# Flamingo gated layer: both kinds of scores in three stretches a step, one pool of two-bank PSUM slots

## The chip, the cores and the metric

The kernel runs on one core of a Trainium2 chip. The metric is the device time of one execution in microseconds; the median of the runs is compared. The core's engines are TensorE (PE, with its weight loads as PEld), VectorE (DVE), ScalarE (ACT), GpSimd (POOL) and SyncE (SP, which issues the DMAs). TensorE writes to PSUM, eight banks of 2 KB on each of 128 partitions; ACT and DVE read it out.

## The reference

A gated layer of cross-attention and a feed-forward part (FFN) with quantised weights, for 32 batches of 224 tokens of width 512, with 750 context tokens of width 384; 16 heads of 32:

```python
q = (x @ Wq.T).reshape(B, N, H, d).transpose(0, 2, 1, 3)
kv = (y @ Wkv.T).reshape(B, N2, 2, H, d).transpose(2, 0, 3, 1, 4)
attn = jnp.einsum('bhnd,bhmd->bhnm', q * scale, k)
attn = jnp.where(pad_mask[:, None, :, None], attn, jnp.float32(-1000000000.0))
attn = jax.nn.softmax(attn, axis=-1)
out = jnp.einsum('bhnm,bhmd->bhnd', attn, v)
...
x = x + jnp.tanh(g_xattn[0]) * _L0_xattn_ref(_layernorm(x, axis=-1), ctx_768, ...)
x = x + jnp.tanh(g_ffn[0]) * _L0_ffn_ref(_layernorm(x, axis=-1), ...)
```

The FFN is two linear layers (512 to 2048 and back) with a GELU between. Before each, the activations are RMS-normalised and rounded to a grid of 127 steps of their row's maximum; the weights are rounded to -1, 0 and 1 times their mean magnitude.

## The kernel before

**Steps.** The attention goes through 128 steps (`steps`, L189): a batch `b` and a group `g` of four heads. The four heads lie on four groups of 32 partitions, so that TensorE can work on the four at once, each with 32 rows of its array.

The softmax needs each row's maximum before the exponential, so the scores are computed twice, in two layouts:
- `maxima(b, g, i)` (L323), i = 0 to 2: scores with queries on the partitions (`sm`), 112 queries by 500 keys for each of four heads. DVE takes the maximum over the keys from PSUM into `mx`. After i = 2, `minus_max` (L350) makes of it the negative maximum in three bf16 parts (`nb`) with six small DVE operations, and `turn_max` (L369) turns these with two transposes on TensorE (`pn`); ACT copies the result to `nT`.
- `weights(b, g, u)` (L380), u = 0 to 2: scores with keys on the partitions (`se`), two chunks of 125 keys by 224 queries for each of four heads. Four small products with ones put the negative maximum into PSUM first, then eight products add the scores. ACT takes the exponential of all four banks in one instruction into `p`; POOL adds up `p` into `acc` (the softmax's denominators over the chunks).

`values` (L413) multiplies `p` with V into `po`, `sums` (L427) adds the denominators beside it, DVE transposes it and takes the reciprocal (`oT`, `rd`), `finish` (L447) scales on POOL and `store` (L488) writes to DRAM (`o_d`) with four DMAs.

**Fillers.** Between the score groups stand other units on TensorE: `k_units` (L275; a half of the K projection each, tile `pk`, read out by ACT), `v_piece` (L291; a piece `pv_None` or half a piece `pv` of the V projection, read out by ACT or DVE), `q_piece` (L262; `pq`, read out by DVE), and the FFN of the tokens that are through with attention: `b_matmul` (tile `ph`, first layer, read out by DVE) and `c_matmul` (tile `po2`, second layer, shown as `po<-w2q,hT`, called c below).

**Slots.** The loop over the steps (L1193) cuts each into six slots k. In an even slot stands `maxima` of the next step, in an odd one `weights` of this step, and after each the units put into that slot: first those marked as quick, then what `Ffn.fill` (L1011) picks from the FFN, then the rest. `fill` takes FFN units, in their order and with minimum distances in slots, as long as estimates of their time on PE, ACT and DVE fit into the slot's room (`PE_ROOM`, L1190). During the first steps `weight_units` (L498) take the place of the FFN: they read the FFN weights and quantise them. What is left of the FFN at the end goes out in an order worked out by `drain` (L1049). Every engine runs its instructions in the order in which this program issues them.

**PSUM.** Two pools share the eight banks:

```python
ps_s = pool("ps_s", 1, PSUM)     # L173: one slot, 4 banks: sm or se
ps_m = pool("ps_m", 4, PSUM)     # L174: four slots, 1 bank: all other units
```

So `sm` and `se` use one slot in turn: each has to wait until the engine that reads the other is through.

Of the kernel before, what the change touches and what calls it, by code (L numbers as in the profile page):

```python
# [9 lines left out]
F32 = mybir.dt.float32  # L10
# [15 lines left out]
def flamingo_gated_layer(  # L26
# [30 lines left out]
    P = 128  # L57
# [112 lines left out]
    smf = pool("smallf", 3)  # L170
    fp = pool("f", 1)
    htp = pool("hT", 2)
    ps_s = pool("ps_s", 1, PSUM)  # L173
    ps_m = pool("ps_m", 4, PSUM)  # L174

    wq_sb = wp.tile([P, NDC, D], F32, name="wq_sb")
# [143 lines left out]
        [(1, MQ, M, 0)],  # L320
    ]

    def maxima(b, g, i):  # L323


        qT, kT = q_of[b], k_of[b, g]
        if i == 0:
            mx_of[b, g] = smp.tile([CP, HG, 4], F32, tag="mx", name=f"mx_{b}_{g}")
        mx = mx_of[b, g]
        s = ps_s.tile([P, HG, 512], F32, tag="s", name=f"sm_{b}_{g}_{i}")  # L330
        for t, lo, hi, col in TAKES[i]:
            for j in range(HG):
                rows = slice(j * DH, (j + 1) * DH)
                pe.matmul(
                    s[:CP, j, col : col + hi - lo],
                    qT[rows, g, t * CP : (t + 1) * CP], kT[rows, lo:hi],
                    start=True, stop=True,
                )
        if i == 1:
            dve.tensor_reduce(  # L340
                mx[:, :, 1:3], s[:CP, :, : 2 * MQ].rearrange("p j (a n) -> p j a n", a=2),
                AX.X, ALU.max,
            )
        else:
            at = 3 * (i // 2)
            dve.tensor_reduce(
                mx[:, :, at : at + 1], s[:CP, :, : 2 * MQ].unsqueeze(2), AX.X, ALU.max
            )

    def minus_max(n):  # L350

# [28 lines left out]
    def weights(b, g, u):  # L380


        qT, kT, nT = q_of[b], k_of[b, g], nT_of[b, g]
        s = ps_s.tile([P, HG, 512], F32, tag="s", name=f"se_{b}_{g}_{u}")
        for j in range(HG):
            pe.matmul(
                s[:KC, j, : 2 * S].rearrange("p (i n) -> p i n", i=2),
                ones3[j * DH : j * DH + 3, :KC],
                nT[j * DH : j * DH + 3, :].unsqueeze(1).to_broadcast([3, 2, S]),
                start=True, stop=False,  # L390
            )
        for i in range(2):
            c = 2 * u + i
            for j in range(HG):
                rows = slice(j * DH, (j + 1) * DH)
                pe.matmul(
                    s[:KC, j, i * S : (i + 1) * S],
                    kT[rows, c * KC : (c + 1) * KC], qT[rows, g, :],
                    start=False, stop=(i == 1),
                )  # L400
# [97 lines left out]
    def weight_units():  # L498
# [27 lines left out]
        def mean():  # L526
            pm = ps_m.tile([P, 512], F32, tag="m", name="pwm")
            pe.matmul(pm[:, 0:2], ones, tot, start=True, stop=True)
            held["pm"] = pm

        def scales():
            pm = held.pop("pm")
# [26 lines left out]
        for n, wi in enumerate(every):  # L559
            def two(n=n, wi=wi):  # L560
                if n + 1 < len(every):
                    fetch(*every[n + 1], "wb")
                if n == 0:
                    scales()
                quantise(*wi)
            units.append(two)
        return units
# [37 lines left out]
    def ffn_units(i):  # L605
# [326 lines left out]
        "top": [[("PE", 0.3), ("ACT", 0.4)]],  # L932
# [15 lines left out]
    LAST = {  # L948
        name: [(NF, at) for at in after.split()]
        for name, after in {  # L950
            "w0": "top", "w1": "w0", "w2": "w1", "val": "", "fin0": "val", "sto0": "fin0",
            "vlast": "w2 val fin0", "fin1": "vlast fin0", "fin2": "vlast fin0",
        }.items()
    }
# [3 lines left out]
    class Ffn:  # L958
# [52 lines left out]
        def fill(self, rooms, stored, newest=False):  # L1011


            rooms, some = list(rooms), False
            rooms[0] += self.late(stored, 0 if rooms[0] >= 0.3 else 2)
            while True:
                if self.next < NF and (self.next + 1) * TG * P <= stored * S:
                    if len(self.parts) <= 2 * TG:
                        self.parts += [[self.next, part] for part in ffn_units(self.next)]
                        self.next += 1  # L1020
                found = next(
                    (
                        (p, u)
                        for p in (self.parts[::-1] if newest else self.parts)
                        for u in p[1]
                        if all(not us or min(us, most) <= room
                               for us, most, room in zip(u[3:6], (0.3, 9.0, 9.0), rooms))
                        and self.ready(p[0], u)
                    ),
                    None,  # L1030
                )
# [6 lines left out]
                some |= unit[3] > 0  # L1038
# [3 lines left out]
            return some  # L1042

        def late(self, stored, more):

# [135 lines left out]
    minus_max(0)  # L1181
    first_k = k_units(*steps[2])
    first_k[0]()

    ffn = Ffn()
    wunits = weight_units()
    LATE = 3
    PE_ROOM = 2.5, 1.9  # L1190
    v_left = [(b, hv, i) for b in range(B) for hv in range(2) for i in range(NKC // 2)]
    V_MORE = {0: 2, 2: 1, 3: 1, 4: 1}
    for n in range(N - 1):  # L1193
        b, g = steps[n]
# [32 lines left out]
        if n in V_MORE:  # L1227
            put_values(V_MORE[n])
        if n == 0:
            put(3, 1.7, lambda: centre(2 * P, D))  # L1230
        if n < 2:
            put(5, 1.5, q0[n + 2])
# [5 lines left out]
        more = b + 1 < B  # L1238
# [8 lines left out]
        if more and g > 1:  # L1247
            put(3, 1.5, qs[2 * g - 4])
            put(5, 1.5, qs[2 * g - 3])
        for k in range(6):  # L1250
            if k % 2 == 0:
                maxima(*nxt, k // 2)
            else:
                if k == 3 and last:
                    finish(*last)
                weights(b, g, k // 2)
            if k == 4:
                minus_max(n + 1)

            used = sum(us for us, _ in slots[k])  # L1260
            early = [unit for us, unit in slots[k] if unit in quick]
            for unit in early:
                unit()
            if wunits:
                if k in (1, 3, 5):
                    wunits.pop(0)()
            else:
                ffn.closing = n == N - 2 and k > 2
                some = ffn.fill(
                    (PE_ROOM[k % 2] - used, (1.1, 2.2)[k % 2], 1.7),  # L1270
                    (n - (k < 5)) // NG if n else 0,
                )
                if k == 0 and not some and lent is not None:

                    v_piece(*lent, 0)
                    slots[4] = [
# [5 lines left out]
                    unit()  # L1282
    last = steps[-2:]
    ffn.drain(
        [("top", 0, None, 0, 0, 0, lambda: turn_max(N - 1))]
        + [(f"w{u}", 0, None, 0, 0, 0, lambda u=u: weights(*last[1], u)) for u in range(3)]
        + [
            (name, 0, None, 0, 0, 0, lambda do=do, at=at: [f(*at) for f in do])
            for name, at, *do in (
# [44 lines left out]
```

## Time and profile before

| | |
|---|---|
| median of 3 runs | 2983.3 us (2980.32 to 2983.55) |
| profiled execution: span | 2983.6 us, granted TensorE clock 0.993 |
| PE busy | 2892.7 us, 97% |
| DVE, ACT, POOL busy | 1737.2, 1414.2, 2084.4 us |
| DMA | 189.80 MB, mean 64 GB/s |
| exponential `p<-se` | 384 times, mean 1663 ns |
| reduction `mx<-sm` | 384 times, mean 2243 ns |

The span is the time from the first to the last instruction of one profiled execution. Matmuls are pipelined and their ends are modelled: each is shown some 0.2 us longer than it holds up the next, so busy PE time hides short waits. The distance between the starts of neighbouring groups in the timeline is the safer measure. A group's line gives: line, engine, operation, output<-inputs, shapes, count, busy time and mean time of one, and the engine's idle time ahead of it with what ended most of it. A wait's line gives: who waited for whom, total us, times, longest. A timeline's line gives start and length in us. Most instructions go through one helper that records their order, so they all carry its line, L53, and the tiles' names tell them apart. An f32 matmul is recorded as two.

### The profile page before, as it was taken

What the parts mean: (1) busy time and instruction counts of PE and PEld (TensorE: products, weight loads), DVE (VectorE), ACT (ScalarE), POOL (GpSimd) and SP (SyncE); (2) the same over time, 40 slices, a digit from 0 to 9 for tenths busy, and PEclk for the clock granted to TensorE, in tenths of its full rate; (3) what the DMA queues carried; (4) which work ended last, traced back from release to release, by engine and by line L of the source; (5) the groups of instructions that cost most, each with busy time, mean ns of one, the idle gap of its engine ahead of it and who ended that gap; (6) DMA issues with size and microseconds to landing.
All of it is one profiled execution on the core that took longest, in us unless ns stands there. A gap on an engine that the chain in (4) does not pass through costs nothing.

```text
span 2983.6 us, 62984 instructions
## 1 busy us (share of the span) xinstructions
PE 2892.7 (97%) x26814; PEld 1840.7 (62%) x26814; DVE 1737.2 (58%) x2616; ACT 1414.2 (47%) x1438; POOL 2084.4 (70%) x2723
## 2 busy tenths in 40 slices
PE   8999999999999999999999999999999999999985
PEld 5666566666666666666666666666666666666653
DVE  5566555555556565555555565655655655556556
ACT  2344454544545455445445454544544554545444
POOL 3566767767766876777667777767767777777675
PEclk9999999999999999999999999999999999999998
DMA  5433222223222222222232212123122132222123
GB/s 148 106 99 98 55 50 73 43 62 75 42 61 61 52 55 73 69 44 48 63 73 47 65 40 80 48 62 74 45 50 62 45 71 67 50 71 48 39 52 78
DMA packets 375785, 189.80 MB, mean 64 GB/s; under 512 B 282160, under 2 KB 339920, under 8 KB 375376
## 3 DMA queue, kind: packets, MB, share of 16 engines
q1 hardware_dynamic: 375504, 185.79, 25.6%
q8 instruction: 209, 3.42, 0.5%
q14 instruction: 72, 0.59, 0.1%
HBM read 119.74 MB, written 29.27 MB: 50 GB/s over the span
## 4 chain that ended last, share of the span: by engine, by line
PE 82%; ACT 10%; POOL 3%; DVE 2%; issue 1%; DMA 1%; POOLq 0%; SPq 0%; ACTq 0%; DVEq 0%
PE po L53 17%; PE pk L53 15%; PE se L53 14%; PE sm L53 13%; PE pv_None L53 8%; ACT p L53 7%; PE pv L53 6%; PE ph L53 6%; PE pq L53 3%; DVE mx L53 2%; ACT L53 2%; POOL acc L53 1%; ACT h L53 1%; PE pn L53 1%; POOL h L53 1%
## 5 line engine op out<-in xcount | busy, mean ns | idle before, releaser
L53 POOL TENSOR_TENSOR acc<-acc,p 125x896 f32<-125x896 f32 x510 | 1066.9, 2092 | 324.8 <-ACT p L53 303.6
L53 DVE TENSOR_REDUCE mx<-sm 112x4 f32<-112x2000 f32 (+1 forms) x384 | 861.2, 2243 | 669.3 <-PE sm L53 669.2
L53 ACT ACTIVATE p<-se 125x1792 f32<-125x1792 f32 x384 | 638.8, 1663 | 760.6 <-PE se L53 706.9
L53 PE MATMUL pk<-y,wkv_sb 128*128 128x375 f32 x1536 | 541.6, 488 | 1.5 <-DMA y<-in_ctxT 1.5
L53 PE MATMUL sm<-kT,qT 32*112 32x500 f32 (+1 forms) x4096 | 426.9, 508 | 31.6 <-ACT p L53 22.7
L53 POOL TENSOR_TENSOR acc<-p 125x896 f32<-125x896 f32 x128 | 268.3, 2096 | 240.3 <-ACT p L53 237.1
L53 PEld LDWEIGHTS pk<-y,wkv_sb 128*128 128x128 f32 x1536 | 279.2, 190 | 175.7 <-issue 36.9
L53 PE MATMUL se<-qT,kT 32*125 32x224 f32 x6144 | 359.9, 348 | 0.0
L53 PE MATMUL po<-p,v 125*32 125x224 f32 x6144 | 317.1, 354 | 0.0
L53 PE MATMUL pv<-wkv_sb,y 128*125 128x256 f32 x1248 | 311.0, 385 | 0.0
L53 PEld LDWEIGHTS se<-qT,kT 32*125 32x125 f32 x6144 | 295.4, 183 | 0.1
L53 PEld LDWEIGHTS sm<-kT,qT 32*112 32x112 f32 x4096 | 159.3, 170 | 190.6 <-ACT p L53 137.6
L53 PEld LDWEIGHTS po<-p,v 125*32 125x32 f32 x6144 | 186.5, 110 | 118.9 <-issue 43.1
L53 PEld LDWEIGHTS pv<-wkv_sb,y 128*125 128x125 f32 x1248 | 223.3, 188 | 52.3 <-issue 17.8
L53 ACT COPY kT<-pk 128x375 f32<-128x375 f32 x256 | 120.1, 469 | 282.0 <-PE pk L53 281.2
L53 PE MATMUL pv_None<-wkv_sb,y 128*125 128x256 f32 x1056 | 250.9, 387 | 0.0
L53 PEld LDWEIGHTS pv_None<-wkv_sb,y 128*125 128x125 f32 x1056 | 191.3, 187 | 88.9 <-issue 59.7
L53 PE MATMUL po<-w2q,hT 128*128 128x256 fp8e4 x1792 | 220.9, 279 | 20.8 <-DMA hT<-hq 20.7
L53 DVE SCALAR_TENSOR_TENSOR h<-ph,qa_am,b_sb 128x512 f32<-128x512 f32 x216 | 158.5, 745 | 137.8 <-PE ph L53 110.3
L53 PE MATMUL ph<-w1q,xT 128*128 128x512 fp8e4 x896 | 224.9, 382 | 6.5 <-DMA xT<-xc 4.2
L53 PE MATMUL pq<-xTb,wq_sb 128*128 128x224 f32 x1024 | 221.4, 359 | 0.4 <-DVE wq_sb L53 0.4
L53 PEld LDWEIGHTS <-hT 128*128 128x128 bf16 x1792 | 171.5, 100 | 72.3 <-issue 27.1
(147 smaller groups left out, 2875.1 us busy)
## 6 DMA issues: line engine op xcount, KB each, us to landing
y<-in_ctxT SPq DMA_DIRECT2D x90, 375.0 KB, 4.4
x<-in_x SPq DMA_DIRECT2D x32, 448.0 KB, 4.1
xTb<-in_xT SPq DMA_DIRECT2D x32, 448.0 KB, 3.7
o_d<-yo SPq DMA_DIRECT2D x508, 28.0 KB, 1.8
xg<-in_x SPq DMA_DIRECT2D x26, 512.0 KB, 3.7
og<-o_d SPq DMA_DIRECT2D x26, 512.0 KB, 4.4
out<-xg SPq DMA_DIRECT2D x52, 256.0 KB, 2.1
wa<-in_w1T SPq DMA_DIRECT2D x8, 512.0 KB, 3.8
```

The lines of the kernel that those rows point to most:

```text
L53: return lambda *args, **kw: tc.keep_in_program_order(build(*args, **kw))
```

## The change

- `ps_s` goes. `ps_m` now has four slots of two banks each, for all of TensorE's outputs; a unit that needs one bank takes a slot of two.
- A score group is two tiles of two heads (`score_tiles`), each with a slot of its own. The products are the same and in the same order of heads; the reduction and the exponential become two instructions each, one for each tile.
- The two kinds of scores stand next to each other: in the even slots `weights` u and directly behind it a `maxima`. These are now i = 1 and 2 of the next step and i = 0 of the step after the next. The odd slots hold fillers alone. So a step has three stretches of se, sm and fillers, where it had six of one score group and fillers.
- `minus_max` of the next step stands in slot 2 and its `turn_max` in slot 4 (before, they stood in slot 4 and in slot 0 of the next step). `values` and `sums` move from slot 2 to slot 1, `finish` from 3 to 2, `store` from 5 to 4, the second K half from 1 to 2.
- The FFN's room on PE is counted for a stretch of two slots (5.2, at most 3.0 a slot) and the room on ACT is 2.2 in even and 1.3 in odd slots. The drain has no `turn_max` any more.

```diff
-    ps_s = pool("ps_s", 1, PSUM)
     ps_m = pool("ps_m", 4, PSUM)
...
+    def score_tiles(name):
+        return [
+            ps_m.tile([P, HG // 2, 512], F32, tag="m", name=f"{name}_{two}") for two in range(2)
+        ]
...
-        s = ps_s.tile([P, HG, 512], F32, tag="s", name=f"sm_{b}_{g}_{i}")
+        s = score_tiles(f"sm_{b}_{g}_{i}")
         for t, lo, hi, col in TAKES[i]:
             for j in range(HG):
                 rows = slice(j * DH, (j + 1) * DH)
                 pe.matmul(
-                    s[:CP, j, col : col + hi - lo],
+                    s[j // 2][:CP, j % 2, col : col + hi - lo],
                     qT[rows, g, t * CP : (t + 1) * CP], kT[rows, lo:hi],
                     start=True, stop=True,
                 )
...
+        for two, part in enumerate(s):
+            heads = slice(2 * two, 2 * two + 2)
+            if i == 1:
+                dve.tensor_reduce(
+                    mx[:, heads, 1:3],
+                    part[:CP, :, : 2 * MQ].rearrange("p j (a n) -> p j a n", a=2), AX.X, ALU.max,
+                )
...
-        act.activation(p.rearrange("p j i n -> p j (i n)"), s[:KC, :, : 2 * S], AF.Exp)
+        for two, part in enumerate(s):
+            act.activation(
+                p[:, 2 * two : 2 * two + 2].rearrange("p j i n -> p j (i n)"),
+                part[:KC, :, : 2 * S], AF.Exp,
+            )
...
+    maxima(*steps[1], 0)
+    turn_max(0)
...
-    PE_ROOM = 2.5, 1.9
+    PE_ROOM = 5.2, 3.0
...
-        nxt = steps[n + 1]
+        ahead = [(n + 1, 1), (n + 1, 2), (n + 2, 0)]
...
-        put(0, 0.2, lambda: turn_max(n), first=True)
+        put(4, 0.2, lambda: turn_max(n + 1), first=True)
         if last:
-            put(2, 2.7, lambda: (values(*last), sums(*last)), first=True)
-            put(5, 0.0, lambda: store(*last), first=True)
+            put(4, 0.0, lambda: store(*last), first=True)
...
-            put(1, 1.9, ks[1])
+            put(2, 1.9, ks[1])
...
+        if last:
+            put(1, 2.9, lambda: (values(*last), sums(*last)))
         for k in range(6):
             if k % 2 == 0:
-                maxima(*nxt, k // 2)
-            else:
-                if k == 3 and last:
+                if k == 2 and last:
                     finish(*last)
                 weights(b, g, k // 2)
-            if k == 4:
-                minus_max(n + 1)
-
-            used = sum(us for us, _ in slots[k])
+                at, i = ahead[k // 2]
+                if at < N:
+                    maxima(*steps[at], i)
+                if i == 2:
+                    minus_max(at)
+                room = PE_ROOM[0] - sum(us for us, _ in slots[k] + slots[k + 1])
...
-                some = ffn.fill(
-                    (PE_ROOM[k % 2] - used, (1.1, 2.2)[k % 2], 1.7),
-                    (n - (k < 5)) // NG if n else 0,
-                )
+                spent = ffn.fill(
+                    (min(room, PE_ROOM[1]), (2.2, 1.3)[k % 2], 1.7),
+                    (n - (k < 4)) // NG if n else 0,
+                )
```

More of the change, by code (lines that the diff above doesn't have):

```diff
@@ L338, in maxima @@
                 )
[L339 to L342, printed above, removed]
-            )
-        else:
[L345 to L348, printed above, removed]
+        for two, part in enumerate(s):
[5 more added lines that the diff above has]
+                )
+            else:
+                at = 3 * (i // 2)
+                dve.tensor_reduce(
+                    mx[:, heads, at : at + 1], part[:CP, :, : 2 * MQ].unsqueeze(2), AX.X, ALU.max
+                )
     def minus_max(n):
@@ L383, in weights @@
         qT, kT, nT = q_of[b], k_of[b, g], nT_of[b, g]
-        s = ps_s.tile([P, HG, 512], F32, tag="s", name=f"se_{b}_{g}_{u}")
+        s = score_tiles(f"se_{b}_{g}_{u}")
         for j in range(HG):
             pe.matmul(
-                s[:KC, j, : 2 * S].rearrange("p (i n) -> p i n", i=2),
+                s[j // 2][:KC, j % 2, : 2 * S].rearrange("p (i n) -> p i n", i=2),
                 ones3[j * DH : j * DH + 3, :KC],
@@ L396, in weights @@
                 pe.matmul(
-                    s[:KC, j, i * S : (i + 1) * S],
+                    s[j // 2][:KC, j % 2, i * S : (i + 1) * S],
                     kT[rows, c * KC : (c + 1) * KC], qT[rows, g, :],
@@ L528, in mean @@
             pe.matmul(pm[:, 0:2], ones, tot, start=True, stop=True)
-            held["pm"] = pm
-        def scales():
-            pm = held.pop("pm")
             dve.tensor_scalar(wmean, pm[:, 0:2], 1.0 / (D * F), 1e-5, ALU.mult, ALU.max)
@@ L562, in two @@
                     fetch(*every[n + 1], "wb")
-                if n == 0:
-                    scales()
                 quantise(*wi)
@@ L931, in flamingo_gated_layer @@
         "c": [[("PE", 1.75), ("DVE", 0.5)]], "out": [[("SP", 2.0)]],
-        "top": [[("PE", 0.3), ("ACT", 0.4)]],
         "w": [[("PE", 1.1), ("ACT", 1.7)]],
@@ L950, in flamingo_gated_layer @@
         for name, after in {
-            "w0": "top", "w1": "w0", "w2": "w1", "val": "", "fin0": "val", "sto0": "fin0",
+            "w0": "", "w1": "w0", "w2": "w1", "val": "", "fin0": "val", "sto0": "fin0",
             "vlast": "w2 val fin0", "fin1": "vlast fin0", "fin2": "vlast fin0",
@@ L1011, in fill @@
         def fill(self, rooms, stored, newest=False):
-            rooms, some = list(rooms), False
+            rooms, spent = list(rooms), 0.0
             rooms[0] += self.late(stored, 0 if rooms[0] >= 0.3 else 2)
@@ L1037, in fill @@
                 unit[6]()
-                some |= unit[3] > 0
+                spent += unit[3]
                 rooms = [room - us for us, room in zip(unit[3:6], rooms)]
@@ L1041, in fill @@
             self.slot += 1
-            return some
+            return spent
         def late(self, stored, more):
@@ L1229, in flamingo_gated_layer @@
         if n == 0:
-            put(3, 1.7, lambda: centre(2 * P, D))
+            put(1, 1.7, lambda: centre(2 * P, D))
         if n < 2:
-            put(5, 1.5, q0[n + 2])
+            put(3, 1.5, q0[n + 2])
+        more = b + 1 < B
+        if more and g > 1:
+            put(3, 1.5, qs[2 * g - 4])
+            put(5, 1.5, qs[2 * g - 3])
         lent = v_left[0] if v_left else None
@@ L1237, in flamingo_gated_layer @@
             put_values(3, 5)
-        more = b + 1 < B
         if more and g == 0:
@@ L1246, in flamingo_gated_layer @@
             put(5, 0.0, lambda: load_xT(b + 1))
-        if more and g > 1:
-            put(3, 1.5, qs[2 * g - 4])
-            put(5, 1.5, qs[2 * g - 3])
+        if last:
+            put(1, 2.9, lambda: (values(*last), sums(*last)))
         for k in range(6):
             if k % 2 == 0:
-                maxima(*nxt, k // 2)
-            else:
-                if k == 3 and last:
+                if k == 2 and last:
                     finish(*last)
                 weights(b, g, k // 2)
-            if k == 4:
-                minus_max(n + 1)
-            used = sum(us for us, _ in slots[k])
+                at, i = ahead[k // 2]
[4 more added lines that the diff above has]
+                room = PE_ROOM[0] - sum(us for us, _ in slots[k] + slots[k + 1])
             early = [unit for us, unit in slots[k] if unit in quick]
@@ L1264, in flamingo_gated_layer @@
             if wunits:
-                if k in (1, 3, 5):
+                if k % 2:
                     wunits.pop(0)()
@@ L1268, in flamingo_gated_layer @@
                 ffn.closing = n == N - 2 and k > 2
-                some = ffn.fill(
-                    (PE_ROOM[k % 2] - used, (1.1, 2.2)[k % 2], 1.7),
-                    (n - (k < 5)) // NG if n else 0,
-                )
-                if k == 0 and not some and lent is not None:
+                spent = ffn.fill(
+                    (min(room, PE_ROOM[1]), (2.2, 1.3)[k % 2], 1.7),
+                    (n - (k < 4)) // NG if n else 0,
+                )
+                room -= spent
+                if k == 0 and not spent and lent is not None:
                     v_piece(*lent, 0)
@@ L1284, in flamingo_gated_layer @@
     ffn.drain(
-        [("top", 0, None, 0, 0, 0, lambda: turn_max(N - 1))]
-        + [(f"w{u}", 0, None, 0, 0, 0, lambda u=u: weights(*last[1], u)) for u in range(3)]
+        [(f"w{u}", 0, None, 0, 0, 0, lambda u=u: weights(*last[1], u)) for u in range(3)]
         + [
```

## The prediction

> **What bounds the kernel now.** I read the busy times first, then what PE waited for, then the costliest groups, then the timeline of one step.
>
> ```profile
> PE 2892.7 (97%) x26814; PEld 1840.7 (62%) x26814; DVE 1737.2 (58%) x2616; ACT 1414.2 (47%) x1438; POOL 2084.4 (70%) x2723
> ...
> L53 DVE TENSOR_REDUCE mx<-sm 112x4 f32<-112x2000 f32 (+1 forms) x384 | 861.2, 2243 | 669.3 <-PE sm L53 669.2
> L53 ACT ACTIVATE p<-se 125x1792 f32<-125x1792 f32 x384 | 638.8, 1663 | 760.6 <-PE se L53 706.9
> ```
>
> TensorE is the bound, and ACT and DVE wait for it: the exponential waits for its scores (706.9 us), the reduction for its own (669.2 us). What can be won is what PE waits for:
>
> ```profile
> PE sm L53 <- ACT p L53: 22.7, 53, 1.9
> PE po L53 <- DMA hT<-hq: 20.7, 4, 12.4
> PE se L53 <- DVE mx L53: 17.5, 26, 2.4
> ```
>
> That is little, but a busy PE hides part of a wait in its modelled ends. The timeline shows the whole of it, as distances from start to start:
>
> ```profile
> 1511.35 1.56 PE L53 MATMUL pv<-wkv_sb,y 128*125 128x256 f32 x6
> 1511.56 1.66 ACT L53 ACTIVATE p<-se 125x1792 f32<-125x1792 f32 x1 [0.61 <-PE se L53]
> ...
> 1513.28 1.11 PE L53 MATMUL sm<-kT,qT 32*112 32x500 f32 x8 [0.36 <-ACT p L53]
> ...
> 1514.32 0.27 PE L53 MATMUL pn<-identb,nb 112*128 112x112 bf16 x2
> 1514.43 1.91 PE L53 MATMUL po<-w2q,hT 128*128 128x256 fp8e4 x16
> ...
> 1541.20 0.41 PE L53 MATMUL se<-nT,ones 3*125 3x448 bf16 x4
> ...
> 1542.29 2.16 PE L53 MATMUL pk<-y,wkv_sb 128*128 128x375 f32 x6
> 1542.50 1.66 ACT L53 ACTIVATE p<-se 125x1792 f32<-125x1792 f32 x1 [0.73 <-PE se L53]
> ...
> 1544.38 1.11 PE L53 MATMUL sm<-kT,qT 32*112 32x250 f32 x16
> 1545.42 2.48 PE L53 MATMUL po<-p,v 125*32 125x224 f32 x48
> 1545.56 2.24 DVE L53 TENSOR_REDUCE mx<-sm 112x8 f32<-112x2000 f32 x1 [4.29 <-PE sm L53]
> ```
>
> A weight-score group se holds PE for 1.10 us (1541.20 to 1542.29), a maximum group sm for 1.04 (1544.38 to 1545.42). Its exponential starts 1.30 us after se starts and takes 1.66; sm may follow 0.05 us later. So with one four-bank slot sm starts no sooner than 1.30 + 1.66 + 0.06 = 3.02 us after se. Where the filler between is a half pv (1.39 us) PE comes at 2.49 and waits 0.54; behind pq (1.61) 0.31; behind pk (1.985) 0.10. Over all starts of the run, the distances beyond the shortest of the same pair add up to 85 us: 23 behind pv, 20 behind pq, 15 behind pk (these 58 are the exponential), and 27 before se and elsewhere, where DVE or ACT was late. 85 us is all that the change can free in waits; the kernel starts with 33 us to the first se and ends with 84 us of drain, neither much touched.
>
> **The change part by part.** A stretch is now se, sm, fillers; I call the three of a step A (with po, the values), B, and C (with pn, the turned maxima). In the order of the built program there are 381 before the drain, and the slots can be read from the waits: the first filler behind sm takes the slot of the first half of se and waits for the first half of its exponential; the second filler takes the other half's. This holds in every stretch. sm, 1.04 us long, is all the cover that is left, where a filler of 1.4 to 2.8 us lay between before.
>
> Half an exponential: copies out of PSUM took 469 ns for 375 elements and 584 for 512, the full exponential 1663 for 1792, all on one line of 0.84 ns an element; so 896 take 0.91 us. ACT instructions that follow each other overlap by 0.1 us (the one at 1504.71 ends at 1506.38, the next starts at 1506.28). From the start of se: first half done at 1.30 + 0.91 = 2.21, the second at 3.02. First filler at 2.27, second not before 3.07.
>
> 1. Stretches A and B (254). Before, PE was through with the two groups at 1.10 + 1.04 = 2.14; now the filler starts at 2.27: +0.13 each, +33 us. The second filler finds its slot free, for the first is pv (1.36: to 3.63), pk (1.9) or ph (0.87: to 3.14). Bounds: 2.20 if the first half of se ends 0.07 sooner, the earliest in the rows (+15 us); 2.40 if ACT does not overlap or a copy stands before (+66).
>
> 2. Stretches C (127). The first filler is always pn, 0.11 us, with which nothing can be hidden: the next (half a pv, a ph, a pv or a c) waits for the second half until 3.07, where before it started at 2.14 + 0.11 = 2.25. +0.82 x 127 = +104 us. Bounds: 0 if that filler's slot were free after all (its wait on ACT stands in the program), +117 without the overlap on ACT. I take 104, from the rows.
>
> 3. The waits of before: the 58 us behind the exponential are gone, as are the 27 us of late engines in their old form: -85.
>
> 4. Changes of tile shape. pk takes 1.985 before a score group and 1.897 before pq, 0.09 less. Half of the 768 entries into scores are gone, those from pk all 250: -22. But po now follows pk in most A stretches (before, sm, which costs nothing there: 1.04 as ahead of other work): 115 x 0.09 = +10. Net -12.
>
> The Trainium skill, TensorEngine Tiling (Array Packing), Tiling Modes, says that a change of tiling mode drains TensorE, while a change of tile does not. Then se followed by sm, both on 32 rows, would save a drain, which the rows bear out as se's 1.10 us against 0.93 for its columns at full rate: 1.96 instead of 2.14 for the pair, 69 us over the run, for the change. By the rule as by the rows the first filler still stands until 2.27, so the sum is the same by both; it would differ only if the exponential were out of the way.
>
> 5. New lateness. The last filler of a stretch must be read out before the second half of the next sm, 1.0 us after se starts; before, four one-bank slots of their own gave it several us. For each stretch I added the DVE rows in program order to 2.18 us (sm's start at 1.0, plus its 1.18 to the reduction): two half reductions of 1.17 (half of 2243 is 1.12, a row of 1024 elements took 1.20), the six small ones of minus_max 1.1 in B, FFN work (reduction hm 1.2, statistics 1.7), read-outs 0.4 to 0.75. Example: B with pk and pq is 2.27 + 1.90 + 1.61 = 5.78 long, so sm's half is due at 6.78; DVE has 4.5 + 1.1 + 1.2 (amax) + 0.6 (reciprocals, qT) = 7.4. Overshoots occur in 71 stretches, 86 us in all; after B the wait of C (0.82) hides part of them, which leaves some 45. ACT, added up likewise with Gelu and its two table loads (4.7 us), overshoots in 22 stretches, 14 us. Partly the same: +50. Bounds: 0, if the rows lie better than in the order (in the run before the reduction nearly always started 1.18 us after sm, so DVE was hardly ever late), and 110, if lateness carries over into the next stretch.
>
> Hidden: the larger work of ACT (384 x 0.16: twice 0.91 against 1.66) and DVE (384 x 0.1) beside 47% and 58% busy engines, apart from point 5. values comes a slot earlier, finish with it, store in slot 4 instead of 5; its four SP issues (2.6 us) and POOL's yo (0.57) move with them, past FFN loads that wait for o_d anyhow. The sums need POOL's last acc add, 7.3 us after C's se; they come at about C's 7.6 plus 7 us, as far as before. pn, q and k pieces move within the step, and qT read by the next sm falls under the 1.0 us of point 5. The drain keeps two ph and two c less (5 us of PE, off its chain of waits), the lead-in gains an sm and pn (1.15): 0.
>
> Sum: 33 + 104 - 85 - 12 + 50 = +90 on the execution's 2983.6, which stands 0.3 above the median. Predicted: 3074 us.
>
> **The rivals.**
> - *The slots come free in time* (faster). If the filler behind pn does not wait, point 2 falls away: 2983.6 + 90 - 104 = 2970. For it: ACT is idle at the end of se (in 95 of 100 cases the exponential started 1.23 to 1.33 us after it). Against: two halves cannot both be through by 2.25 when the first starts at 1.30. It decides if C's wait is under (104 - 90) / 127 = 0.11 us.
> - *Nothing is late* (point 5 at its lower end): 3074 - 50 = 3024. For it: DVE and ACT work half the time. Against: the short B stretches, 5.5 to 5.8 us with 7 us of DVE work.
> - *Lateness carries over* (a new bound by DVE and ACT in place of the old wait): point 5 at 110 and the first filler at 2.40 (33 more): 3074 + 60 + 33 = 3167. For it: each late read-out delays sm, and so the next reduction. Against: C's wait gives the engines time each step.
> - *The split does nothing*, the halves being ready together: the second filler's time is then the first's too, +0.8 x 254 = 203 more, 3277; each half is a tile of its own, so I hold it for unlikely.
>
> **How the numbers follow.** Measurement tells about 0.2%, 6 us, from no change. Chances: forecast (3040 to 3105) 0.48; nothing late (2990 to 3040) 0.20; carried over (3105 to 3190) 0.20; slots free 0.08, of which 0.01 within 0.2%; the split does nothing 0.02; several bounds at their lower ends together, no change, 0.02. So faster 0.07, same 0.03, slower 0.90. The range leaves out the faster case and the upper part of the carried-over one: 2995 to 3150.
>
> **What would show it.** Right: in the PE waits, pv, ph, c and pk behind sm or pn wait for ACT p, about 0.8 us each behind pn; sm no longer waits for ACT p of its own stretch; 768 exponentials of 0.91 us and as many reductions of 1.1 to 1.2; steps near 23.3 us on average instead of 22.6 (2866 us from the first se to the drain, over 127). Point 5: sm waits for DVE v, qT or oT. Wrong: no idle PE between pn and its follower; an exponential that starts later than 1.4 us after se in many stretches (then ACT's order, not the slots, is the cause); or a drain that differs by more than 15 us.

## The result, and the profile after

The changed kernel takes 3069.1 us (median of 4 runs, 3067.3 to 3071.4) beside 2981.9 for the kernel before in the same session: 1.029 of its time, 95% interval 1.028 to 1.031. The forecast was 3074. The profiled execution spans 3068.0 us, before 2983.6.

The page of the changed kernel: the busy engines, and the groups of the halved reduction and exponential (busy time, mean ns of one, idle time ahead):

```profile
PE 2859.9 (93%) x26814; PEld 1917.6 (63%) x26814; DVE 1775.7 (58%) x2987; ACT 1436.1 (47%) x1868; POOL 2082.8 (68%) x2735
...
L53 DVE TENSOR_REDUCE mx<-sm 112x2 f32<-112x1000 f32 (+1 forms) x768 | 886.3, 1196 | 521.9 <-PE sm L53 521.3
...
L53 ACT ACTIVATE p<-se 125x896 f32<-125x896 f32 x768 | 662.1, 915 | 891.9 <-PE se L53 889.0
```

PE has the same 26814 instructions and is busy for 33 us less in a span that is 84 us longer. ACT and DVE have hardly more to do; ACT still waits for PE for half of the span (1516 us), DVE for 1166 us. The new time is idle time of PE, and the waits of PE name its cause (total us, times, longest):

```profile
PE pv L53 <- ACT p L53: 41.3, 118, 0.8
PE ph L53 <- ACT p L53: 31.0, 95, 0.6
PE pn L53 <- ACT p L53: 19.7, 85, 0.6
PE pk L53 <- ACT p L53: 19.6, 87, 0.5
...
PE sm L53 <- DVE v L53: 11.6, 10, 1.4
...
PE sm L53 <- DVE qT L53: 9.6, 15, 2.1
```

Before, sm waited for the exponential of its own slot. Now the fillers wait for it. The timeline of one C stretch shows where (start, length):

```profile
1518.86 0.41 PE L53 MATMUL se<-nT,ones 3*125 3x448 bf16 x4
...
1519.86 1.01 PE L53 MATMUL sm<-kT,qT 32*112 32x500 f32 x8
...
1520.07 1.73 ACT L53 ACTIVATE p<-se 125x896 f32<-125x896 f32 x2 [3.89 <-PE se L53]
...
1521.04 0.26 PE L53 MATMUL pn<-identb,nb 112*128 112x112 bf16 x2 [0.17 <-ACT p L53]
...
1521.84 1.91 PE L53 MATMUL po<-w2q,hT 128*128 128x256 fp8e4 x16 [0.55 <-ACT p L53]
```

se starts at 1518.86 and sm 1.00 us later, without a wait. Both are through on PE by about 1520.9, but pn starts at 1521.04, 2.18 after se, when the first half of the exponential has given its slot back. pn covers 0.11 us, so the next filler stands until 2.98, when the second half is through. ACT had waited for 3.89 us before this exponential: it isn't busy, the fillers come too soon behind the scores.

From such distances, start to start, the 84 us can be split. I took all 380 stretches from the first se on. For each kind of unit and follower the shortest distance seen in the two kernels counts as its own work, what is beyond it as idle time. The own work of the pair se and sm is taken as 2.14 us in both, so the row of own work is that of the other units alone:

```
                                       before    after    us
up to the first se                       32.9     31.1    -1.8
380 stretches: units' own work           1949     1924   -25
               waits of the kind before                  -97   (57 ahead of sm, 23 ahead of se,
                                                               17 else)
               first filler behind sm                     +91   (39 exponential's first half,
                                                               28 exponential late, 24 sm late)
               filler behind pn                           +78
               other fillers, and ahead of se             +37   (some 15 second fillers)
what follows them                        92.2     95.0    +2.8
```

The stretches' rows are rounded; together they went from 2858.5 to 2941.9 us. The parts in brackets are read off stretch by stretch and are good to a few us.

### The profile page after: what moved, and what is told of

Its sections match the earlier page's. It is cut to its first block, busy times and chain, and to the rows that moved or that the text cites. A ratio compares the mean times of both kernels' runs of the same rounds, so it can differ in the third digit from the quotient of the medians.

```text
span 3068.0 us, 63863 instructions
## 1 busy us (share of the span) xinstructions
PE 2859.9 (93%) x26814; PEld 1917.6 (63%) x26814; DVE 1775.7 (58%) x2987; ACT 1436.1 (47%) x1868; POOL 2082.8 (68%) x2735
## 4 chain that ended last, share of the span: by engine, by line
PE 76%; ACT 15%; POOL 3%; DVE 2%; issue 2%; DMA 1%; SPq 0%; POOLq 0%; ACTq 0%; DVEq 0%
PE po L53 17%; PE pk L53 15%; ACT p L53 13%; PE se L53 13%; PE pv L53 12%; PE ph L53 6%; PE pq L53 6%; PE pv_None L53 5%; PE sm L53 1%; POOL acc L53 1%; DVE mx L53 1%; ACT h L53 1%; DVE wb L53 1%; POOL r_a L53 1%; ACT L53 0%
## 5 line engine op out<-in xcount | busy, mean ns | idle before, releaser
L53 DVE TENSOR_REDUCE mx<-sm 112x2 f32<-112x1000 f32 (+1 forms) x768 | 886.3, 1196 | 521.9 <-PE sm L53 521.3
L53 ACT ACTIVATE p<-se 125x896 f32<-125x896 f32 x768 | 662.1, 915 | 891.9 <-PE se L53 889.0
L53 PE MATMUL pv<-wkv_sb,y 128*125 128x256 f32 x1716 | 429.5, 388 | 41.4 <-ACT p L53 41.3
L53 PE MATMUL sm<-kT,qT 32*112 32x500 f32 (+1 forms) x4096 | 418.9, 479 | 33.4 <-DVE v L53 11.6
L53 PEld LDWEIGHTS pv<-wkv_sb,y 128*125 128x125 f32 x1716 | 310.1, 188 | 134.8 <-ACT p L53 80.7
L53 DVE STREAM_TRANSPOSE oT<-po 128x448 f32<-128x448 f32 x128 | 83.2, 650 | 290.0 <-PE po L53 290.0
L53 PEld LDWEIGHTS sm<-kT,qT 32*112 32x112 f32 x4096 | 197.4, 171 | 68.1 <-DVE v L53 20.5
L53 POOL TENSOR_TENSOR yo<-oT,rd 128x224 f32<-128x224 f32 x127 | 72.4, 570 | 241.7 <-DVE rd L53 241.5
L53 PE MATMUL pq<-xTb,wq_sb 128*128 128x224 f32 x1024 | 214.8, 353 | 0.4 <-DVE wq_sb L53 0.4
L53 PEld LDWEIGHTS pq<-xTb,wq_sb 128*128 128x128 f32 x1024 | 190.9, 190 | 16.9 <-DVE wq_sb L53 1.1
```

Of the source, the lines that this page charges most:

```text
L53: return lambda *args, **kw: tc.keep_in_program_order(build(*args, **kw))
```

## The experiments

Two theories: **the wait** (W), that the time goes into fillers which wait for the exponential of the score pair just ahead of them; and **lateness** (L), that ACT and DVE, which run their instructions in order, are late with something else, so that taking this wait away gives little. Other rivals are named in the expectations. All ratios are to the kernel before, run again beside each (2982 to 2985 us).

**turn5: the turned maxima a slot later**, so that a longer filler stands ahead of pn.

```diff
-        put(4, 0.2, lambda: turn_max(n + 1), first=True)
+        put(5, 0.2, lambda: turn_max(n + 1), first=True)
```

> The changed kernel with turn_max of the next step in slot 5 instead of 4: pn is no longer the first filler behind sm in stretch C, a longer unit is. Theory W (PE waits for the halves of the exponential, whose slots the two fillers behind sm take; most of it behind pn): the 0.8 us that the filler behind pn waits are covered by a filler of 0.87 us or more in some 120 of 127 steps, 120 x 0.8 = 96 us less, about 2973 us; in C the second filler starts 3.1 to 3.7 us after se without a wait for ACT p. Rival L (DVE and ACT come late, and the wait behind pn is only where they catch up): the time comes back as waits of sm for DVE v, qT and ACT kT; less than 40 us are gained, 3030 or more.

Measured: 3048.1 us, 1.021 (1.020 to 1.023). The wait behind pn went as W had it, from 78 us to 4, and the time fell by 21 only. That is the time that L named (3030 or more), but the place is another: not sm is late, but se. It stands in the timeline:

```profile
819.89 0.26 PE L53 MATMUL pn<-identb,nb 112*128 112x112 bf16 x2
...
820.56 1.91 ACT L53 ACTIVATE h<-h 128x2048 f32<-128x2048 f32 x1
822.49 1.28 ACT L53 ACT_TABLE_LOAD   x1
...
824.14 0.35 ACT L53 COPY nT<-pn 128x224 bf16<-128x224 bf16 x1
...
824.54 0.41 PE L53 MATMUL se<-nT,ones 3*125 3x448 bf16 x4 [3.04 <-ACT nT L53]
```

pn runs on PE at 819.89. Its copy nT stands on ACT behind a Gelu with its table loads, and se needs nT. The trace has 27 waits of se for nT, 55.6 us. In slot 4 the copy has the next slot's time as cover, in slot 5 none.

**pool_alone: the pool without the new order.** Before's six stretches, with the shared pool of four two-bank slots and the halves:

```diff
-    ps_s = pool("ps_s", 1, PSUM)
     ps_m = pool("ps_m", 4, PSUM)
...
+    def score_tiles(name):
+        return [
+            ps_m.tile([P, HG // 2, 512], F32, tag="m", name=f"{name}_{two}") for two in range(2)
+        ]
```

> The kernel before with the change's pool alone: four two-bank slots for all of TensorE, scores in two tiles, reductions and exponentials in halves; the six stretches and the order of all units stay as before (the mean of the weights is read out in the same unit, as in the change). Theory W: fillers of 1.4 us and more stand between se and sm, the next sm takes a free slot and the slot of se's first half (free 2.27 us after se) or, behind two fillers, both halves' (3.07); the 58 us that sm waited for the whole exponential go, part of the other 27 too: about 2925 us (2905 to 2945), faster than both kernels. Rival P (the shared two-bank slots or the halving cost time by themselves): 2982 or more, and PE waits behind the read-outs of fillers.

Measured: 3012.4 us, 1.009 (1.008 to 1.011), where W had a gain; the rival P holds. The waits of sm for the exponential did fall (behind pv from 23 us to 4, behind pq from 20 to 7), but the distances beyond the shortest grew from 85 us to 124 in all. The score halves now take slots that fillers had. In its timeline the first half of an se goes and the second waits:

```profile
1258.40 2.16 PE L53 MATMUL pk<-y,wkv_sb 128*128 128x375 f32 x6
...
1261.63 1.91 ACT L53 ACTIVATE h<-h 128x2048 f32<-128x2048 f32 x1
...
1264.31 0.40 PE L53 MATMUL se<-nT,ones 3*125 3x448 bf16 x2
...
1264.96 0.45 ACT L53 COPY kT<-pk 128x375 f32<-128x375 f32 x1
...
1265.47 0.40 PE L53 MATMUL se<-nT,ones 3*125 3x448 bf16 x2 [0.75 <-ACT kT L53]
```

The second half's slot is that of pk, before sm and the values. PE was through with pk at about 1260.5, but ACT reads it out only at 1264.96, behind a Gelu and its table loads.

**halves_own: the halves without the shared pool.** As pool_alone, but the scores have two slots of two banks and the fillers their four of one:

```diff
-    ps_s = pool("ps_s", 1, PSUM)
+    ps_s = pool("ps_s", 2, PSUM)
```

> The kernel before with halved scores, reductions and exponentials, but no shared slots: two slots of two banks for the scores alone, four of one bank for the fillers as before. Tells the price of halving from that of sharing. Theory S (sharing: a filler's late read-out holds up scores and other fillers): the extra waits of the version with the shared pool go, and those for the exponential come back, the second half of sm being free 3.07 us after se instead of 3.02: 2985 (2975 to 3000). Rival H (halving itself costs: more ACT and DVE work, a group of four products cut in two): 3005 or more, as with the shared pool (3012).

Measured: 2981.3 us, 0.9989 (0.9979 to 0.9998). Cutting the exponential and the reduction in two costs nothing and brings nothing; the 27 us of pool_alone are the sharing. Why it brings nothing shows behind a pv that follows se: sm now starts 2.59 us after se instead of 3.02, but its second half stands until 3.10, when the second half of the exponential is through, and the unit behind starts at 4.07, before at 4.06.

**sm_first: the maxima ahead of the weights in each stretch**, so that the fillers take the slots of sm and wait for DVE.

```diff
-                weights(b, g, k // 2)
                 at, i = ahead[k // 2]
                 if at < N:
                     maxima(*steps[at], i)
+                weights(b, g, k // 2)
```

> The changed kernel with sm ahead of se in each stretch. Theory W: the two fillers behind the pair now take the slots of sm and wait for the halves of its reduction. Its first half starts 1.05 us after sm and takes 1.20, so the first filler starts at 2.31 from the pair's start (now 2.24), the second not before 3.5 (now 3.05): 381 x 0.07 + 127 x 0.45 behind pn + 69 x 0.3 behind a single ph = 27 + 57 + 21 = 105 us more, about 3174 (3130 to 3215), and PE waits for DVE mx in place of ACT p. Rival A (ACT's load or order is the cause, not the slot): these waits fall away and nothing takes their place, 3069 or less.

Measured: 3248.1 us, 1.088 (1.086 to 1.090), 74 us over what was expected. The waits turned to the other engine:

```profile
PE pv L53 <- DVE mx L53: 75.0, 126, 0.9
PE ph L53 <- DVE mx L53: 45.9, 95, 0.8
```

The first filler starts 2.40 us after the pair (2.31 expected), the one behind pn at 3.50 (3.5). So the fillers wait for whichever engine reads the pair's first group. Of the surplus, the first filler's 0.09 us in 380 stretches make 34 us. The rest is lateness: sm and se wait 63 us for qT, v and kT, where the changed kernel has 25, and PE ran 75 us of the stretches at half clock, where it has 31 (last section).

**pad_act: 0.18 us more in front of every exponential.**

```diff
+    pad = wp.tile([P, P], F32, name="pad")
...
+        act.copy(pad[:KC], s[0][:KC, 0, :P])
         for two, part in enumerate(s):
```

> The changed kernel with one small ACT instruction ahead of each pair of exponentials, a copy of 128 elements from the first half of se; its result is not used. It takes about 0.28 us, 0.1 of which overlaps, so both halves come about 0.18 us later; ACT's busy share goes from 47 to 50%. Theory W: every first filler (381) stands 0.18 us later: 69 us more, about 3138 (3120 to 3160). Rival L (what counts is how much work ACT has in the short stretches): only those 22 stretches in which ACT overshoots feel it, under 10 us, 3079 or less.

Measured: 3140.2 us, 1.052 (1.050 to 1.054): 71 us over the changed kernel, 69 expected. 71 over 380 stretches is 0.19 each, and the first filler's typical start moved from 2.24 to 2.40. ACT is 47% busy, and yet a copy of 265 ns in front of each exponential lies on PE's path in nearly every stretch. That is W, and lateness of other work, which would have left slack here, falls as the main cause.

**pn_second: the turned maxima behind a V piece in slot 4**, the other way to cover pn.

```diff
+            ahead_of = [unit for us, unit in slots[k] if k == 4 and us > 1 and unit not in quick][:1]
+            for unit in ahead_of:
+                unit()
             early = [unit for us, unit in slots[k] if unit in quick]
...
-                if unit not in quick:
+                if unit not in quick and unit not in ahead_of:
                     unit()
```

> The changed kernel with turn_max left in slot 4, but behind that slot's piece of V and ahead of the FFN: in C a piece of V is the first filler, pn the second, and the copy to nT stands ahead of the FFN's work on ACT. With turn_max in slot 5 the wait behind pn fell from 77 to 4 us, but se waited 56 us for nT, whose copy stood behind Gelu. Theory W (slots of the exponential, behind pn): the 77 us go without that new wait: 3069 - 77 = 2992 (2975 to 3010). Rival L (engines are late and the time comes back elsewhere whatever stands behind sm): 3030 or more, with waits of se or sm in its place.

Measured: 3091.0 us, 1.036 (1.034 to 1.037), slower than the change. The wait behind pn is gone (0 us). In its place the exponentials come later (on the mean 1.46 us after se, 1.35 in the changed kernel; 15 of them stand directly behind the Gelu block and are 42 us late together), and some 20 reductions stand behind late V read-outs (about 50 us). One place in the timeline:

```profile
1168.78 1.91 ACT L53 ACTIVATE h<-h 128x2048 f32<-128x2048 f32 x1
...
1170.04 0.41 PE L53 MATMUL se<-nT,ones 3*125 3x448 bf16 x4
...
1172.12 0.35 ACT L53 COPY v<-pv 125x256 f32<-125x256 f32 x1
...
1172.37 1.73 ACT L53 ACTIVATE p<-se 125x896 f32<-125x896 f32 x2
1172.52 1.10 PE L53 MATMUL sm<-kT,qT 32*112 32x250 f32 x12 [0.90 <-ACT v L53]
```

The exponential starts 2.33 us after its se, behind the Gelu and the V copy; three quarters of sm's products (x12 of the records) wait for that copy's slot. So W is right on what the change lost, and L on what can be won back: the wait behind pn was also what gave ACT and DVE time to catch up.

**after_flat, pn_second_flat: is it the Gelu?** Its place on ACT is taken by a plain pass of the same size without table loads. These kernels, and the other two with `flat` in their names, leave the Gelu out until the drain.

```diff
-            act.activation(h, h, AF.Gelu)
-            if not draining:
-                act.activation(warm, magic, AF.Exp)
+            act.activation(h, h, AF.Gelu if draining else AF.Identity)
```

> The changed kernel with the FFN's Gelu replaced by a plain copy of the same size until the drain; so the two table loads (1.28 us each) and the small exponential that loads the table back are left out, and ACT's Gelu block falls from 4.7 to 1.9 us (50 times). The output is not the layer's. Theory G (after the slots of the exponential, the rest of the lateness is the Gelu block, which stands in ACT's order ahead of the next exponentials and copies): the exponentials, which start 1.35 us after se on the mean, come back to the usual 1.27 (29 us), with a few late copies: 3069 - 35 = 3034 (3020 to 3048). Rival D (DVE's read-outs behind the reductions are late): within 15 us of 3069.

> The same with pn behind the piece of V (pn_second, 3091 us, where the wait behind pn was gone and the exponentials of A came up to 4 us late). Theory G: there the copy to nT waits for the later pn, with Gelu queued behind it on ACT, and so the next step's exponentials; without the block the 77 us behind pn are won at last: 3034 - 77 = 2957 (2940 to 2990). Rival D: 3070 or more.

Measured: 3061.4 us, 1.026 (1.025 to 1.028), and 3026.8, 1.015 (1.013 to 1.017). In the changed kernel the Gelu costs 8 us, so there D, the rival that sets it under 15 us, holds. With pn second it costs 64 (3091 to 3027), which neither theory had; and with the Gelu flat, covering pn wins 35 us (3061 to 3027) of the 77 that were expected of it in the changed kernel (3069 to 2992). 24.5 us of sm waiting for V read-outs on DVE remain.

**pn_second_flat_v: the V pieces read out by ACT alone**, besides.

```diff
-        if i % 2:
-            dve.tensor_copy(to[:, part], pv[:KC, part])
-        else:
-            act.copy(to[:, part], pv[:KC, part])
+        act.copy(to[:, part], pv[:KC, part])
```

> pn_second_flat (3027 us: pn behind the piece of V, Gelu a plain copy until the drain, so the output is not the layer's), with all pieces of V read out by ACT and none by DVE. Without the wait behind pn it won 35 us over after_flat (3061) and not 77; in its trace sm's second half waits 24.5 us for DVE v, and 21 of its reductions start late behind a read-out of V (29 us). Theory D (DVE's read-out of the last filler, queued behind reductions and FFN work, takes the rest): it goes with it, 3027 - 35 = 2992 (2975 to 3010). Rival A (ACT's 107 further copies of 0.37 to 0.58 us come just as late): 3020 or more, sm waiting for ACT v.

Measured: 2992.1 us, 1.003 (1.002 to 1.005), as D had it. No wait of sm for V on DVE is left. Against after_flat it is 69 us, most of the 77. After_flat with V on ACT was not run, so the parts aren't strictly apart. Still, the order of the queues on ACT and DVE accounts for nearly all of what pn_second failed to win.

**eight_pairs, eight_six: slots of one bank.** Eight slots of one bank, each score group four tiles, in the changed order and in the order before. The first diff is for both (against the kernel before `ps_s` goes too):

```diff
-    ps_m = pool("ps_m", 4, PSUM)
+    ps_m = pool("ps_m", 8, PSUM)
...
-            ps_m.tile([P, HG // 2, 512], F32, tag="m", name=f"{name}_{two}") for two in range(2)
+            ps_m.tile([P, 512], F32, tag="m", name=f"{name}_{j}") for j in range(HG)
...
-        for two, part in enumerate(s):
-            act.activation(
-                p[:, 2 * two : 2 * two + 2].rearrange("p j i n -> p j (i n)"),
-                part[:KC, :, : 2 * S], AF.Exp,
-            )
+        for j, part in enumerate(s):
+            act.activation(p[:, j].rearrange("p i n -> p (i n)"), part[:KC, : 2 * S], AF.Exp)
```

> The changed kernel with eight slots of one bank for all units, scores in four tiles of one head, reductions and exponentials in quarters. From the halves (915 against 1663 ns whole, 1196 against 2243) a quarter exponential takes 0.54 us, a quarter reduction 0.67. Theory W: the first quarter is free 1.27 + 0.54 + 0.05 = 1.86 us after se, before PE is through with the pair (1.00 + 1.04), so the first filler starts at 2.04 instead of 2.24, the second at 2.30 instead of 3.05 behind pn: 381 x 0.20 + 127 x 0.55 = 146 us less, 2923; with 0.3 us more of DVE work a stretch in the some 70 short ones 2945 (2910 to 2970). Rival L (DVE and ACT are late): both have more work than in halves, so 3050 or more.

> The kernel before, six stretches and its order, with the same eight slots of one bank and quarters. Theory S (slots): sm finds four slots free or soon free, a filler takes one bank and not two, so twice as many units lie between a read-out and the next use of its slot; the 47 us of waits for the exponential go and the some 80 us that the four shared slots added do not come: 2945 (2920 to 2975). Rival H: quarters cost more than halves, and sharing is sharing: above 3012.

Measured: eight_pairs 2989.8 us, 1.0019 (1.0009 to 1.0030), 20 us above W's range and 60 below L's; eight_six 2944.6, 0.987 (0.985 to 0.988), as expected and the fastest of all. In eight_pairs the first filler typically starts at 1.94 us, sooner than expected (2.04), and the one behind pn at 2.30, as expected, but exponentials are late by 0.13 us on the mean against their typical start (0.08 in the changed kernel), and sm waits for read-outs:

```profile
PE sm L53 <- DVE v L53: 21.4, 16, 2.1
...
PE sm L53 <- DVE qT L53: 17.4, 14, 2.5
```

In eight_six only 0.9 us of these waits is left. Its timeline, with sm behind a q piece:

```profile
1502.64 0.41 PE L53 MATMUL se<-nT,ones 3*125 3x448 bf16 x4
...
1503.74 1.78 PE L53 MATMUL pq<-xTb,wq_sb 128*128 128x224 f32 x8
1503.83 1.85 ACT L53 ACTIVATE p<-se 125x448 f32<-125x448 f32 x4 [4.44 <-PE se L53]
1505.45 1.11 PE L53 MATMUL sm<-kT,qT 32*112 32x500 f32 x8
```

sm starts 2.81 us after se and waits for nothing, though the exponential ends at 1505.68: before, it could start at 3.02 at the earliest.

**eight_pairs_flat**, eight_pairs with the flat Gelu:

> The same with eight one-bank slots and quarters (eight_pairs, 2990 us, exponentials 1.38 us after se on the mean, usually 1.25). Theory G: 381 x 0.12 = 47 us and a few late copies less: 2935 (2915 to 2955). Rival D: 2975 or more.

Measured: 2974.2 us, 0.997 (0.995 to 0.999), 16 us less than eight_pairs. That is at D's bound (2975) and far above G's range: the Gelu isn't what holds it.

Together, medians in us:

```
                                       six stretches   three pairs
scores' own slot, fillers' four             2981            -
four shared slots of two banks              3012          3069
eight shared slots of one bank              2945          2990
```

In both rows that have both, the new order costs, 57 and 45 us, and the two-bank slots cost 67 and 79 more than those of one bank. With one bank the read-outs come in quarters too; no run takes the size of the slots and that of the read-outs apart.

## Why the prediction was right, and where its terms were not

The time was right to 5 us in 3069, and its cause was: the fillers wait for the exponential's halves. But its terms were mis-sized and nearly cancel: the new lateness was 39 us more than predicted, the other four together 46 us less. That the sum came out within 5 us is luck in this part.

1. *First filler in A and B, +33*: it starts at 2.24 typically, not 2.27. 254 x 0.10 = +25.
2. *C behind pn, +104*: the second filler starts at 3.05 typically (3.07 predicted). The first filler's 0.10 in 127 stretches and 78 us behind pn make +91. Pad_act and turn5 show that both waits are for the exponential.
3. *The waits of before, -85*: -97. Of the 58 us that I read as waits for the exponential, some 32 were. Behind pk 0.10 us is no wait: the distance to sm is the same, 2.089 us, in pool_alone, halves_own and eight_six, whose exponentials are through sooner. There, 42 of the 126 pv and 62 of the 124 pq ahead of sm also stand 0.10 above the shortest, so 24 of the 58 us are this step. Its cause stays open; pk ahead of pq, a unit on the full array, has it too (1.894 or 1.998 us). Late engines made up the rest and more.
4. *Changes of tile shape, -12*: -25. The K pieces came out nearly as counted (-14). The V pieces were not counted: a whole one took 2.784 us up to se, 85 times, and takes 2.59 to 2.69 ahead of the units that follow it now, and a half one takes 1.388 up to se or sm and as little as 1.30 elsewhere (together -16). The FFN's pieces are some 5 us more.
5. *New lateness, +50*: +89. 24 late second halves of sm, 28 late exponentials, 37 at other fillers and ahead of se. The sum of DVE rows in the B stretches found the first; the exponentials were missed. What stands on ACT just ahead of the late ones in the trace is a read-out of V (10 times, 11 us), the quantising of the FFN weights in the first steps (4, 11 us), a read-out of kT (10, 5 us) and the Gelu block (once, 3 us). I let ACT count only where its sum overshot a stretch, but an exponential can be late in a stretch with room to spare, if what stands ahead of it in the queue is issued late.

The Trainium skill, TensorEngine Tiling (Array Packing), Tiling Modes, says that a change of mode drains TensorE. The pair of se and sm agrees with it. se takes 0.999 us up to sm, where it took 1.097 up to a filler; in eight_pairs, where the filler behind need not wait, sm takes 0.94 instead of 1.04. So the pair takes 1.94 us there, 1.96 by the prediction's columns and 2.14 before. In the changed kernel this wins nothing, as predicted, because the filler stands until 2.24 anyway.

Of the hidden work: the drain came out 2.8 us longer (within the 15 allowed), the lead-in 1.8 shorter, and the halves cost what was read from the copies' line (915 ns for 0.91; 1196 for the reduction, 1.17 predicted); halves_own shows that they are free. The mean stretches are 8.61 (A), 6.81 (B) and 7.81 us (C), a step of 23.2, with 23.3 predicted and 22.6 before. An exponential that starts later than 1.4 us after its se, the sign of ACT's order as the cause, is in 26 of 380 stretches.

The rivals: *slots free in time* falls by the wait of C. *The split does nothing* falls as the first and second filler start 0.8 apart. *Nothing is late* falls by the 89 us. *Lateness carries over* is near the truth in kind, but not in size; it shows its full weight where the wait behind pn is taken away (turn5, pn_second).

## What to carry to other kernels

When a buffer's users are put closer together, find the first unit that takes each slot after the last write, and count what lies between: here the two slots come free 2.2 and 3.0 us after the start of se, and se and sm cover 2.04 of it, where before a filler of 1.4 to 2.8 us stood between as well; and a unit as short as pn covers nothing for the next. A wait that can be seen is worth no more than the time to the next late engine: taking 78 us of waits away gave 21 in turn5 and cost 22 in pn_second, because ACT and DVE run in order and the copy or exponential stood behind a Gelu or a read-out (and, in part, by the clock, next section). Slots of the size of the smallest unit (eight of one bank, read out in quarters) were worth 67 to 79 us, and gained 1.3% without any change of order.

## What was not expected of the hardware

The granted clock falls to half in periods of 3.41 us or two or three of them. In the 380 stretches there are 2 such periods before (13.7 us in all), 8 in the changed kernel (30.7 us), 16 in turn5 (71.7), 21 in pn_second (102.4), 11 in pn_second_flat (41.0), 4 in pn_second_flat_v (13.7), 17 in eight_pairs (64.8) and 2 in eight_six (6.8). They start at multiples of 3.41 us from each other, so I divided the stretches of all 14 traces into windows in that step and added up PE's idle time in each (by the modelled ends). Windows at full clock with 1.8 us and more were always followed by half clock (70 of 70), those with 1.2 to 1.8 us at times (51 of 115), and those with less hardly ever (10 times, the least at 0.87). At half rate at most half of the period is lost, so up to 15 us in the changed kernel, 7 before and 51 in pn_second; of the 64 us that flattening the Gelu won there, up to 31 can be the clock. Undisturbed groups take as long before and after (the values' group po 2.785 us from start to start in both), so it isn't a slower clock throughout. So a kernel with several idle gaps close to each other pays for them again, and part of what is called lateness above is this; no run here takes the two apart.

The Trainium skill, TensorE: Matmul & The Clock Gate, HAM oscillation, gives the rule of no idle gaps over about 3.4 us. Here less was enough: idle time that adds up to 1.2 to 1.8 us within a window at times, 1.8 us and more always. The measurement decides.
